# Two quantised feed-forward weights prepared in quarters instead of whole, in a four-stage transformer kernel

## The chip, the cores and the metric

The kernel runs on one core of a Trainium2 chip. A core has a matrix engine (TensorE, PE in the profile; its weight loads are PEld), a vector engine (VectorE, DVE), an activation engine (ScalarE, ACT), a general engine (GpSimd, POOL) and a queue that issues DMAs (SyncE, SP). Each engine works through its own queue in order and waits on semaphores for the others. The metric is the device time of one execution in microseconds (us); lower is better. Before the change the median of three runs is 962.21 us (961.23 to 963.15).

## What is computed

Four stages run over x of shape (8, 512, 256), each with a residual and a layer norm:

```python
x = layernorm(x + retention(x, past_kv, W_qkv, ...))         # 16 heads, group norm
x = layernorm(x + ffn(x, W_fc, ln_w, ln_b, W_proj))          # the change is here
x = layernorm(x + linear_attention(x, Wq, Wk, Wv, ...))
x = layernorm(x + mixture_of_experts(x, w_router, wi, wo))

def absmean(W):                          # W_fc is (1024, 256), W_proj is (256, 1024)
    gamma = mean(abs(W)) + 1e-6
    return sign(W / gamma) * minimum(round(abs(W / gamma)), 1)      # -1, 0 or 1

def ffn(x, W_fc, ln_w, ln_b, W_proj):
    h = gelu(x @ absmean(W_fc).T)
    h = layernorm(h, ln_w, ln_b)
    return h @ absmean(W_proj).T
```

Before feed-forward can run, each of its weights is summed in absolute value over all its elements (for gamma), turned into -1, 0 and 1 by two thresholds at half of gamma, and transposed. W_proj is also scaled by ln_w, has its column means taken away, and gives a bias from ln_b: the layer norm is folded into the weight.

## The kernel before, in words

One batch has 512 tokens in four blocks (chunks) of 128. Its retention stage is `stage_a1`, group norm and residual `stage_a2`, feed-forward `stage_b` and `stage_bn`, linear attention `stage_c1` and `stage_c2`; experts follow for two groups of four batches. The stages of different batches are interleaved.

The order is not written by hand. Every stage is a generator, and `interleave` advances the one whose next step may begin first by a planned clock. `op(engine, cost, t, ...)` enters an instruction with a cost and the time at which its inputs are expected; it is placed in the first free stretch of that engine's planned time. Two engine names matter here: `DVS` is VectorE working from SBUF only, for which the planner also books a "port" that `POOL` books too; `DVE` books VectorE alone. `pe(cost)` advances the planned time of TensorE, `need(t)` waits in the plan until `t`, and `later(t)` hands on a time. The planned times set the order of the instructions in each engine's queue, and nothing else: on the chip the semaphores decide. Where the plan leaves TensorE idle for over 1.4 us, `interleave` enters spare matmuls on the identity and a table (line 294), whose output nobody reads.

The preparation of feed-forward is the generator `prepare_ffn`, which runs beside `stage_a1` of batch 0. It issues one DMA of 1 MB for W_fc into one half of the tile `prepare`, one for W_proj into `pr_w`, and two for ln_w and ln_b (`lnwb`, line 678). `threshold` plans the arrival by its last argument (24.0 and 27.0 us), sums the whole weight by one VectorE reduction into a column `fc_t` or `pr_t`, adds over the partitions by a matmul with ones (line 647) and makes the two thresholds by three small instructions (lines 651 to 655). `ternary` makes the quantised weight by two VectorE instructions over 128x2048 elements: a compare (`is_lt`) and a compare with a subtraction (`is_gt`, `subtract`). Then come 16 transposes of each weight on TensorE (line 692 `fc_tp`, line 705 `pr_tp`) with copies by ScalarE, the product with ln_w on VectorE (`prT`), the bias (`pr_bias`, line 721), the means (`pr_mean`, line 729) and the subtraction of the means from `prT` on VectorE.

In `stage_a1` of a batch, TensorE makes q and k (`qk_ps`, line 880) and v (`v_ps`, line 904), and then for each of the four chunks: scores (`sc`, line 928), a transpose of k (`kd_tp`, line 935), the chunk's output (`r_ps`, lines 948 to 961) and the state's update (`st_ps`, line 970). Between the scores and the output stands the decay mask: three of four score banks are multiplied on VectorE and one is copied by ScalarE and multiplied on POOL (`masked`, tiles `scm`). `past_bd`, the state carried in, is made by four VectorE instructions (lines 612 and 617) and `gnp`, the spread group-norm weights, by four more (lines 623 and 624). The last chunk's statistics (`gn_st`) begin `stage_a2`. `stage_a1` of batch 1, whose first instructions on TensorE are the transposes of x at line 348, comes after that of batch 0 and after `prepare_ffn`. `prepare_l1`, the generator behind it, transposes the weights of the third stage (line 801, `l_tp`), clears two padding tiles on POOL (`pad`) and issues small DMAs.

DMAs are all on SP's queue, in the order of the plan. At the start they are: identity, x of batch 0, wqkv, the tables `cst`, `past`, two for `gn`, W_fc, W_proj, two for `lnwb`, x of batch 1, four small vectors of the third stage and the first of its weights.

Of the kernel before, what the change touches and what calls it, by code (L numbers as in the profile page):

```python
# [11 lines left out]
F32 = mybir.dt.float32  # L12
# [3 lines left out]
ALU = mybir.AluOpType  # L16
AX = mybir.AxisListType
# [3 lines left out]
P = 128  # L21
B, S, D = 8, 512, 256
NC = S // P
NK = D // P
# [57 lines left out]
def tile_layers(ctx: ExitStack, tc: tile.TileContext, ins, out, at):  # L82
# [6 lines left out]
    def bc(ap, axis, n):  # L89

        shape = list(ap.shape)
        return ap.unsqueeze(axis).to_broadcast(shape[:axis] + [n] + shape[axis:])
# [83 lines left out]
    def op(engine, cost, t, fn, *args, use=None, drop=None, bank=None, **kw):  # L176


        if engine in (GELU, EXP):
            cost += 0.0 if engine == Plan.loaded else TABLE  # L180
            engine, Plan.loaded = ACT, engine
        users = [engine]
        if engine in (DVS, POOL):
            users.append("port")
        engine = users[0] = {DVS: DVE, POOLD: POOL}.get(engine, engine)
        t = t + HOP
        if use is not None:
            t = max(t, take(use) + HOP)
        if engine != SP:
            length = max(cost - OVERLAP[engine], 0.05)  # L190
            found = False
            while not found:
                found = True
                for user in users:
                    for a, b in Plan.busy[user]:
                        if t + length <= a:
                            break
                        if b > t:
                            t, found = b, False
            for user in users:  # L200
                bisect.insort(Plan.busy[user], (t, t + length))
                while Plan.busy[user][0][1] < Plan.t - 30.0:
                    Plan.busy[user].pop(0)
        Plan.count += 1
        heapq.heappush(Plan.events, (t, Plan.count, lambda: fn(*args, **kw)))  # L205
        t += cost
        if drop is not None:
            give(drop, t)
        if bank is not None:
            release(bank, t)  # L210
        return t
# [5 lines left out]
    def pe(cost):  # L217


        start = max(Plan.now, Plan.t)  # L220
        if start - Plan.now > 1.5:
            Plan.slow = start + (1.5 if start - Plan.now < 3.0 else 8.0)
        cost += min(max(Plan.slow - start, 0.0) / 2, cost)
        Plan.now = Plan.t = start + cost
        return Plan.now + PE_OUT
# [12 lines left out]
    def need(t, n=1):  # L238

        while True:  # L240
            r = max(t + HOP_PE, sorted(Plan.banks)[n - 1] + HOP if n else 0.0)
            yield "pe", r if r < HELD else Plan.t + 0.5
            if not n or sorted(Plan.banks)[n - 1] <= Plan.t + 1e-6:
                return
# [324 lines left out]
    with ExitStack() as stages:  # L569
# [15 lines left out]
        def dma(t, out, in_):  # L585
            op(SP, 0.0, t, nc.sync.dma_start, out=out, in_=in_)
# [49 lines left out]
        prbias = fb.tile([P, D], F32, name="prbias")  # L636
        lnwb = fb.tile([P, 2, NF], F32, name="lnwb")

        def threshold(name, w, t):

            tot = fb.tile([P, 1], F32, name=f"{name}_t")
            t = op(
                DVE, 2.3, t, V.tensor_reduce, tot, w, AX.X, ALU.add, apply_absolute_value=True
            )
            yield from need(t)
            ps = bank(f"{name}_ps")
            T.matmul(ps[:, 0:1], ones, tot, start=True, stop=True)
            half = fb.tile([P, 2], F32, name=f"{name}_h")

            def halves():  # L650
                nc.vector.tensor_scalar(
                    half[:, 1:2], ps[:, 0:1], 1.0 / (FF * D), 1e-6, ALU.mult, ALU.add
                )
                nc.vector.tensor_scalar(half[:, 0:1], half[:, 1:2], 0.5, None, ALU.mult)
                nc.vector.tensor_scalar(half[:, 1:2], half[:, 1:2], -0.5, None, ALU.mult)

            return half, op(DVE, 0.5, pe(0.2), halves, bank=ps)

        def ternary(q, w, half, t):
            t = op(DVS, 1.3, t, V.tensor_scalar, q, w, half[:, 1:2], None, ALU.is_lt)  # L660
            return op(
                DVS, 2.35, t, V.scalar_tensor_tensor, q, w, half[:, 0:1], q, ALU.is_gt, ALU.subtract
            )

        def prepare_ffn():

            big = fb.tile([P, 2, FF * D // P], F32, tag="big", bufs=1, name="prepare")
            w_fc, q_fc = (big[:, i].rearrange("p (n c) -> p n c", n=NF) for i in range(2))
            dma(0.0, w_fc, ins["L0_ffn_W_fc"].rearrange("(n p) c -> p n c", p=P))
            w_pr, q_pr = (  # L670
                wk.tile([P, NK, FF], F32, tag="b8", bufs=B8, name=f"pr_{i}") for i in "wq"
            )
            dma(0.0, w_pr, ins["L0_ffn_W_proj"].rearrange("(m p) c -> p m c", p=P))

            def vectors():
                for j, k in enumerate(("L0_ffn_ln_w", "L0_ffn_ln_b")):
                    with nc.allow_non_contiguous_dma(reason="a vector of 1024, once"):
                        nc.sync.dma_start(
                            out=lnwb[:, j, :], in_=ins[k].rearrange("(n p) -> p n", p=P)
                        )  # L680

            op(SP, 0.0, 0.0, vectors)
            half, t = yield from threshold("fc", big[:, 0], 24.0)
            ready = ternary(big[:, 1], big[:, 0], half, t)
            half, t = yield from threshold("pr", w_pr.rearrange("p m c -> p (m c)"), 27.0)
            ready_pr = ternary(*(x.rearrange("p m c -> p (m c)") for x in (q_pr, w_pr)), half, t)
            for k in range(NK):
                for n4 in range(NF // 4):
                    yield from need(ready)
                    ps = bank("fc_tp")  # L690
                    for n in range(4):
                        T.transpose(
                            ps[:, n * P : (n + 1) * P],
                            q_fc[:, n4 * 4 + n, k * P : (k + 1) * P], ident,
                        )
                    fc_done = op(
                        ACT, 0.6, pe(0.46), A.copy, fcT[:, k, n4 * 512 : (n4 + 1) * 512], ps, bank=ps
                    )
            raw = big[:, 0].rearrange("p (f d) -> p f d", f=NF)
            for n2 in range(NF // 2):  # L700
                yield from need(ready_pr)
                ps = bank("pr_tp")
                for n in range(2):
                    for m in range(NK):
                        T.transpose(
                            ps[:, (n * 2 + m) * P : (n * 2 + m + 1) * P],
                            q_pr[:, m, (n2 * 2 + n) * P : (n2 * 2 + n + 1) * P], ident,
                        )
                t = op(
                    ACT, 0.6, pe(0.46), A.copy,  # L710
                    raw[:, n2 * 2 : n2 * 2 + 2, :].rearrange("p n d -> p (n d)"), ps, bank=ps,
                )
            give("b8", Plan.now, 2)
            w = op(
                DVS, 2.3, t, V.tensor_tensor, prT[:, :, :D], raw, bc(lnwb[:, 0, :], 2, D), ALU.mult
            )
            op(DVE, 0.1, w, V.memset, prT[:, :, D : D + 1], 1.0 / FF)
            yield from need(t)
            acc = bank("pr_bias")
            for f in range(NF):  # L720
                T.matmul(
                    acc[:, :D], lnwb[:, 1, f : f + 1].to_broadcast([P, P]), raw[:, f, :],
                    start=(f == 0), stop=(f == NF - 1),
                )
            op(ACT, 0.4, pe(3.5), A.copy, prbias, acc[:, :D], bank=acc)
            yield from need(w)
            acc = bank("pr_mean")
            for f in range(NF):
                T.matmul(acc[:, :D], ones, prT[:, f, :D], start=(f == 0), stop=(f == NF - 1))
            mean = wk.tile([P, D], F32, tag="ex", bufs=EX, name="pr_mean_s")  # L730
            t = op(
                ACT, 0.4, pe(3.5), A.activation, mean, acc[:, :D], AF.Copy, scale=1.0 / FF,
                use="ex", bank=acc,
            )
            t = op(
                DVS, 2.3, t, V.tensor_tensor, prT[:, :, :D], prT[:, :, :D], bc(mean, 1, NF),
                ALU.subtract, drop="ex",
            )
            yield later(t)
            return t  # L740

# [1078 lines left out]
```

## Time and profile before

| what | value |
|---|---|
| median of three runs | 962.21 us |
| profiled execution, time | 959.53 us |
| profiled execution, span in the trace | 957.8 us |
| mean granted clock of TensorE | 0.977 |
| busy in 0 to 24 us: PE, DVE, ACT, POOL | 18.38, 6.49, 5.97, 8.21 us |
| busy in 24 to 48 us: PE, DVE, ACT, POOL | 22.68, 20.65, 7.32, 5.78 us |
| busy in 60 to 100 us (40 us): PE, DVE | 38.85, 21.14 us |
| spare matmuls in the whole span | 164 passes, 43.3 us |

The span is what the trace covers; the time of the same execution is 1.7 us longer. A matmul of 32-bit floats appears as two passes in the rows, so "x12" spare rows are six instructions. In a timeline a row gives the start in us from the span's start, how long the group lasted, the engine, the line, the operation, the tiles written and read, the shape, the number of instructions and, in brackets, how long the engine stood idle before it and what released it. L205 is the line of the helper that enters a planned instruction, so the tile names say which it is. A row of the DMA issues ends in the size and the time from issue to landing.

### The profile page before, as it was taken

The numbers are of one execution on the slowest core, as the hardware profiler recorded it, in microseconds if no ns is written. First come the engines' busy times: TensorE is split into PE (matmuls) and PEld (weight loads), VectorE is DVE, ScalarE is ACT, GpSimd is POOL, SyncE is SP. The second block draws the span as 40 slices with busy tenths as digits, with TensorE's granted clock in tenths as the row PEclk, the third lists the DMA queues.
The fourth block names the chain that finished last, engine by engine and source line by source line (L and its number), as shares of the span: only waits on it lengthen the run. The fifth ranks groups of instructions, "written<-read, shape, count | busy, mean of one in ns | idle before, by whom it ended". The sixth has DMA issues, their size and how long they took to land. (4 is left out here: it accounts for less than half of the span.)

```text
span 957.8 us, 18818 instructions
## 1 busy us (share of the span) xinstructions
PE 902.4 (94%) x7704; PEld 706.9 (74%) x7704; DVE 614.9 (64%) x1506; ACT 445.2 (46%) x862; POOL 397.2 (41%) x404
## 2 busy tenths in 40 slices
PE   7999999999999998999998999979999999999892
PEld 4777777777777786777676766658686898999891
DVE  2855446788668678767889788857765953513224
ACT  2337266356834943671755155632655534122213
POOL 3246446432554543362436134362365223253333
PEclk9999999999999999999999899989999999999895
DMA  6030000002000100200020010001503356339742
GB/s 209 8 111 2 2 1 2 2 1 67 1 2 23 46 1 1 67 2 1 1 68 1 1 43 4 2 1 45 190 15 108 122 172 207 80 92 369 244 123 101
DMA packets 49542, 60.68 MB, mean 63 GB/s; under 512 B 5585, under 2 KB 44689, under 8 KB 49457
## 3 DMA queue, kind: packets, MB, share of 16 engines
q1 hardware_dynamic: 45600, 53.92, 16.9%
q0 software_dynamic: 3856, 5.57, 3.0%
q8 instruction: 60, 0.98, 0.4%
q14 instruction: 26, 0.20, 0.1%
HBM read 43.76 MB, written 15.73 MB: 62 GB/s over the span
## 5 line engine op out<-in xcount | busy, mean ns | idle before, releaser
L1125 PE MATMUL pr_ps<-prT,fT 128*128 128x257 f32 x512 | 117.1, 382 | 0.3 <-ACT scm L205 0.3
L1125 PEld LDWEIGHTS pr_ps<-prT,fT 128*128 128x128 f32 x512 | 95.5, 189 | 16.6 <-issue 1.9
L205 POOL TENSOR_TENSOR fsq<-fsq,fsf 128x512 f32<-128x512 f32 x56 | 72.6, 1296 | 30.6 <-ACT fsf L205 28.1
L1517 PE MATMUL wo_ps<-e_hT,wo 128*128 128x160 f32 x512 | 75.2, 305 | 0.0
L1488 PE MATMUL wi_ps<-xsT,wi 128*128 128x160 f32 x512 | 74.8, 300 | 0.0
L205 ACT ACTIVATE e_hT<-wi_ps 128x480 f32<-128x480 f32 (+1 forms) x48 | 25.3, 527 | 105.4 <-PE wi_ps L1488 105.4
L1517 PEld LDWEIGHTS wo_ps<-e_hT,wo 128*128 128x128 f32 x512 | 71.9, 193 | 1.1 <-issue 0.6
L1488 PEld LDWEIGHTS wi_ps<-xsT,wi 128*128 128x128 f32 x512 | 70.7, 190 | 0.5 <-issue 0.2
L205 DVE TENSOR_TENSOR hm<-hs,cst 128x512 f32<-128x512 f32 x96 | 60.0, 676 | 15.6 <-PE hs L1264 15.6
L205 POOL TENSOR_TENSOR ln_rs<-ln_rs,mhalf 128x4 f32<-128x4 f32 x32 | 33.4, 1045 | 84.2 <-DVE ln_rs L205 84.2
L205 POOL TENSOR_TENSOR scm<-scm,cst 128x512 f32<-128x512 f32 x32 | 43.7, 1367 | 54.2 <-ACT scm L205 54.1
L205 DVE TENSOR_TENSOR scm<-sc,cst 128x512 f32<-128x512 f32 x96 | 60.1, 676 | 8.6 <-PE sc L928 8.6
L1205 PE MATMUL qk_ps<-l1T,x2T 128*128 128x512 f32 x128 | 61.7, 603 | 0.0
L205 POOL TENSOR_TENSOR hm<-hm,cst 128x512 f32<-128x512 f32 x32 | 40.9, 1279 | 48.2 <-ACT hm L205 48.2
L205 DVE STREAM_TRANSPOSE hT<-pad 128x512 f32<-128x512 f32 x64 | 59.3, 958 | 2.1 <-ACT pad L205 1.4
L205 POOL DMA_INDIRECT y_d<-eo,srci x21 | 32.5, 1549 | 66.2 <-ACT eo L205 33.5
L880 PE MATMUL qk_ps<-xT,wqkv 128*128 128x512 f32 x128 | 59.4, 606 | 0.0
L1096 PE MATMUL fc_ps<-x1T_l,fcT 128*128 128x512 f32 x128 | 53.2, 415 | 2.8 <-DVE x1T_l L205 1.5
L1096 PE MATMUL fc_ps<-x1T_h,fcT 128*128 128x512 f32 x128 | 50.2, 392 | 0.0
L205 ACT ACTIVATE x<-x,ln_nb,ln_rs 128x256 f32<-128x256 f32 x64 | 33.2, 589 | 31.5 <-DVE ln_nb L205 31.4
L294 PE MATMUL spare<-cst,cst_ident 128*128 128x256 f32 x164 | 43.3, 415 | 0.0
L205 ACT ACT_TABLE_LOAD x33 | 42.3, 1283 | 1.3 <-PEq L1806 0.7
(257 smaller groups left out, 1990.2 us busy)
## 6 DMA issues: line engine op xcount, KB each, us to landing
wi<-in_L_ffn_wi SPq DMA_DIRECT2D x13, 1024.0 KB, 6.7
wo<-in_L_ffn_wo SPq DMA_DIRECT2D x13, 1024.0 KB, 7.6
x<-in_L_attn_x SPq DMA_DIRECT2D x8, 512.0 KB, 3.9
x_d<-a SPq DMA_DIRECT2D x8, 512.0 KB, 3.0
y_d<-a SPq DMA_DIRECT2D x8, 512.0 KB, 4.1
z<-y_d SPq DMA_DIRECT2D x8, 512.0 KB, 6.2
out<-z SPq DMA_DIRECT2D x8, 512.0 KB, 3.1
prepare<-in_L_ffn_W_fc SPq DMA_DIRECT2D x1, 1024.0 KB, 11.3
```

The source lines that it names most:

```text
L205: heapq.heappush(Plan.events, (t, Plan.count, lambda: fn(*args, **kw)))
L294: T.matmul(ps[:, :256], ident, cst[:, :256], start=True, stop=True)
L880: T.matmul(ps, wqkv[:, k, which * D + m * P : which * D + (m + 1) * P], xT[:, k, :], start=(k == 0), stop=(k == NK - 1),)
L1096: T.matmul(ps, fcT[:, k, f * P : (f + 1) * P], x[:, k, :], start=(k == 0 and x is low), stop=(k == NK - 1 and x is high),)
L1125: T.matmul(acc[:, : D + 1], hT[:, f, c * P : (c + 1) * P], prT[:, f, :], start=(f == 0), stop=(f == NF - 1),)
L1205: T.matmul(qk, x2T[:, k, cs], l1T[:, k, 0:2, :].rearrange("p a d -> p (a d)"), start=(k == 0), stop=(k == NK - 1),)
L1488: T.matmul(ps[:, f * CAP : (f + 1) * CAP], wi[:, k, (f3 + f) * P : (f3 + f + 1) * P], x[:, k, es], start=(k == 0), stop=(k == NK - 1),)
L1517: T.matmul(ps[:, m * CAP : (m + 1) * CAP], wo[:, f, m * P : (m + 1) * P], hT[:, f, :], start=(f == 0), stop=(f == NF - 1),)
```

## The change

W_fc is loaded by four DMAs of 256 KB (two blocks of 128 rows each) and W_proj by four (half a row block each). Each quarter is summed by a reduction of its own into one of four columns, and the sum over partitions accumulates four matmuls with ones instead of one. The quantising runs as four pairs of 128x512 instructions, the product with ln_w and the subtraction of the means as four instructions each. The planned arrivals are 12.0, 13.5, 14.7 and 16.0 us for the quarters of W_fc (24.0 for the whole before) and 17.0 to 20.0 for W_proj (27.0 before); costs in the plan are cut accordingly. The transposes of W_fc run block of four first, and each waits in the plan for the quarter that it reads.

Because the plan decides the order, the built queues differ as follows, all in the first two batches. TensorE: the sums of W_fc stand before `v_ps` instead of behind the first chunk's spare matmuls; the sums of W_proj and the transposes of W_fc stand behind the first chunk's scores, the transposes of W_proj behind the second's; bias and means stand before the third chunk's scores instead of the fourth's; one block of third-stage transposes stands before batch 1's x transposes. Spare instructions by chunk are 2, 0, 6 and 5 instead of 6, 5, 5 and 7, and 2 are added in batch 1. VectorE: three sums of W_fc stand before `past_bd`, the fourth before `kT`, all of W_fc's quantising and the sums of W_proj before the first masks. SP: the eight quarter DMAs stand in place of the two.

```diff
--- before.py
+++ after.py
@@ -636,15 +636,20 @@
         prbias = fb.tile([P, D], F32, name="prbias")
         lnwb = fb.tile([P, 2, NF], F32, name="lnwb")
 
-        def threshold(name, w, t):
-
-            tot = fb.tile([P, 1], F32, name=f"{name}_t")
-            t = op(
-                DVE, 2.3, t, V.tensor_reduce, tot, w, AX.X, ALU.add, apply_absolute_value=True
-            )
+        def threshold(name, parts, ts):
+
+            tot = fb.tile([P, len(parts)], F32, name=f"{name}_t")
+            for i, (part, t) in enumerate(zip(parts, ts)):
+                t = op(
+                    DVE, 0.61, t, V.tensor_reduce, tot[:, i : i + 1], part, AX.X, ALU.add,
+                    apply_absolute_value=True,
+                )
             yield from need(t)
             ps = bank(f"{name}_ps")
-            T.matmul(ps[:, 0:1], ones, tot, start=True, stop=True)
+            for i in range(len(parts)):
+                T.matmul(
+                    ps[:, 0:1], ones, tot[:, i : i + 1], start=(i == 0), stop=(i == len(parts) - 1)
+                )
             half = fb.tile([P, 2], F32, name=f"{name}_h")
 
             def halves():
@@ -654,23 +659,37 @@
                 nc.vector.tensor_scalar(half[:, 0:1], half[:, 1:2], 0.5, None, ALU.mult)
                 nc.vector.tensor_scalar(half[:, 1:2], half[:, 1:2], -0.5, None, ALU.mult)
 
-            return half, op(DVE, 0.5, pe(0.2), halves, bank=ps)
-
-        def ternary(q, w, half, t):
-            t = op(DVS, 1.3, t, V.tensor_scalar, q, w, half[:, 1:2], None, ALU.is_lt)
-            return op(
-                DVS, 2.35, t, V.scalar_tensor_tensor, q, w, half[:, 0:1], q, ALU.is_gt, ALU.subtract
-            )
+            return half, op(DVE, 0.5, pe(0.5), halves, bank=ps)
+
+        def ternary(qs, ws, half, t):
+
+            ends = []
+            for q, w in zip(qs, ws):
+                e = op(DVS, 0.36, t, V.tensor_scalar, q, w, half[:, 1:2], None, ALU.is_lt)
+                ends.append(op(
+                    DVS, 0.64, e, V.scalar_tensor_tensor, q, w, half[:, 0:1], q, ALU.is_gt,
+                    ALU.subtract,
+                ))
+            return ends
 
         def prepare_ffn():
 
             big = fb.tile([P, 2, FF * D // P], F32, tag="big", bufs=1, name="prepare")
             w_fc, q_fc = (big[:, i].rearrange("p (n c) -> p n c", n=NF) for i in range(2))
-            dma(0.0, w_fc, ins["L0_ffn_W_fc"].rearrange("(n p) c -> p n c", p=P))
             w_pr, q_pr = (
                 wk.tile([P, NK, FF], F32, tag="b8", bufs=B8, name=f"pr_{i}") for i in "wq"
             )
-            dma(0.0, w_pr, ins["L0_ffn_W_proj"].rearrange("(m p) c -> p m c", p=P))
+            fc_rows = ins["L0_ffn_W_fc"].rearrange("(n p) c -> p n c", p=P)
+            pr_rows = ins["L0_ffn_W_proj"].rearrange("(m p) c -> p m c", p=P)
+            fours = range(4)
+            for i in fours:
+                dma(0.0, w_fc[:, 2 * i : 2 * i + 2], fc_rows[:, 2 * i : 2 * i + 2])
+
+            def half_row(x, i):
+                return x[:, i // 2, i % 2 * 512 : (i % 2 + 1) * 512]
+
+            for i in fours:
+                dma(0.0, half_row(w_pr, i), half_row(pr_rows, i))
 
             def vectors():
                 for j, k in enumerate(("L0_ffn_ln_w", "L0_ffn_ln_b")):
@@ -680,13 +699,15 @@
                         )
 
             op(SP, 0.0, 0.0, vectors)
-            half, t = yield from threshold("fc", big[:, 0], 24.0)
-            ready = ternary(big[:, 1], big[:, 0], half, t)
-            half, t = yield from threshold("pr", w_pr.rearrange("p m c -> p (m c)"), 27.0)
-            ready_pr = ternary(*(x.rearrange("p m c -> p (m c)") for x in (q_pr, w_pr)), half, t)
-            for k in range(NK):
-                for n4 in range(NF // 4):
-                    yield from need(ready)
+            parts = [[big[:, k, i * 512 : (i + 1) * 512] for i in fours] for k in range(2)]
+            half, t = yield from threshold("fc", parts[0], [12.0, 13.5, 14.7, 16.0])
+            ready = ternary(parts[1], parts[0], half, t)
+            parts = [[half_row(w, i) for i in fours] for w in (w_pr, q_pr)]
+            half, t = yield from threshold("pr", parts[0], [17.0, 18.0, 19.0, 20.0])
+            ready_pr = max(ternary(parts[1], parts[0], half, t))
+            for n4 in range(NF // 4):
+                for k in range(NK):
+                    yield from need(ready[2 * n4 + 1])
                     ps = bank("fc_tp")
                     for n in range(4):
                         T.transpose(
@@ -711,9 +732,11 @@
                     raw[:, n2 * 2 : n2 * 2 + 2, :].rearrange("p n d -> p (n d)"), ps, bank=ps,
                 )
             give("b8", Plan.now, 2)
-            w = op(
-                DVS, 2.3, t, V.tensor_tensor, prT[:, :, :D], raw, bc(lnwb[:, 0, :], 2, D), ALU.mult
-            )
+            for f in range(0, NF, 2):
+                w = op(
+                    DVS, 0.62, t, V.tensor_tensor, prT[:, f : f + 2, :D], raw[:, f : f + 2],
+                    bc(lnwb[:, 0, f : f + 2], 2, D), ALU.mult,
+                )
             op(DVE, 0.1, w, V.memset, prT[:, :, D : D + 1], 1.0 / FF)
             yield from need(t)
             acc = bank("pr_bias")
@@ -732,10 +755,12 @@
                 ACT, 0.4, pe(3.5), A.activation, mean, acc[:, :D], AF.Copy, scale=1.0 / FF,
                 use="ex", bank=acc,
             )
-            t = op(
-                DVS, 2.3, t, V.tensor_tensor, prT[:, :, :D], prT[:, :, :D], bc(mean, 1, NF),
-                ALU.subtract, drop="ex",
-            )
+            for f in range(0, NF, 2):
+                e = op(
+                    DVS, 0.62, t, V.tensor_tensor, prT[:, f : f + 2, :D], prT[:, f : f + 2, :D],
+                    bc(mean, 1, 2), ALU.subtract, drop="ex" if f == NF - 2 else None,
+                )
+            t = e
             yield later(t)
             return t
 
```

## Prediction

> **What bounds the kernel now.** I read the page's busy shares first, then the timeline of all engines over the first 60 us (the change touches nothing later), then the DMA issues with their time to landing, and last the places where TensorE waited. The first line says which engine to follow:
>
> ```profile
> PE 902.4 (94%) x7704; PEld 706.9 (74%) x7704; DVE 614.9 (64%) x1506; ACT 445.2 (46%) x862; POOL 397.2 (41%) x404
> ```
>
> TensorE is the bound, so the change is worth what it moves TensorE's queue by the time the second batch begins (the x transposes at 56.81), since from there on the queues of both programs are almost the same. But "busy" includes spare matmuls, which only pass time. Timeline:
>
> ```profile
> 18.69 1.15 PE L928 MATMUL sc<-qz,kT 32*128 32x256 f32 x16
> 20.05 2.76 PE L294 MATMUL spare<-cst,cst_ident 128*128 128x256 f32 x12
> 20.51 2.27 DVE L205 TENSOR_REDUCE fc_t<-prepare 128x1 f32<-128x2048 f32 x1
> 24.45 1.29 DVE L205 TENSOR_SCALAR prepare<-prepare,fc_h 128x2048 f32<-128x2048 f32 x1
> 25.77 2.35 DVE L205 SCALAR_TENSOR_TENSOR prepare<-prepare,fc_h 128x2048 f32<-128x2048 f32 x1
> 27.01 2.32 PE L294 MATMUL spare<-cst,cst_ident 128*128 128x256 f32 x10
> 30.47 0.35 PE L647 MATMUL pr_ps<-pr_t,cst 128*128 128x1 f32 x2 [1.13 <-DVE pr_t L205]
> 36.45 2.32 PE L294 MATMUL spare<-cst,cst_ident 128*128 128x256 f32 x10
> 51.13 2.29 DVE L205 TENSOR_TENSOR prT<-prT,pr_mean_s 128x2048 f32<-128x2048 f32 x1 [5.60 <-ACT pr_mean_s L205]
> 51.69 2.89 PEld L294 LDWEIGHTS spare<-cst,cst_ident 128*128 128x128 f32 x14 [0.33 <-issue]
> 52.50 2.06 POOL L205 TENSOR_TENSOR scm<-scm,cst 128x512 f32<-128x512 f32 x1 [11.94 <-ACT scm L205]
> 56.81 1.09 PE L348 MATMUL tp<-cst_ident,x 128*128 128x128 f32 x8
> ```
>
> The reader should see four gaps, one behind each of the four score blocks, filled by 46 spare passes of 0.23 us (10.7 us) plus 1.13 us of plain waiting: that is the reserve a better order could use. The DMA issues say when the weights are there:
>
> ```profile
> prepare<-in_L_ffn_W_fc SPq DMA_DIRECT2D x1, 1024.0 KB, 11.3
> pr_w<-in_L_ffn_W_proj SPq DMA_DIRECT2D x1, 1024.0 KB, 13.3
> gn<-in_L_attn_gn_weight SPq DMA_DIRECT2D x1, 8.0 KB, 8.6
> gn<-in_L_attn_gn_bias SPq DMA_DIRECT2D x1, 8.0 KB, 8.8
> ```
>
> Issued at 4.29 and 4.77, they land at 15.6 and 18.1, and VectorE takes them at 20.51 and 28.04. The slack is 5 to 10 us; the change spends it.
>
> **The loads.** Two DMAs become eight. In the compiled order each hardware DMA waits for the landing of the one eight issues earlier. So the four fc quarters leave at 4.3, 4.8, 5.4 (x landed) and 7.3 (wqkv landed, 1.64+5.6), the pr quarters at 9.1, 9.6, 11.8 and 12.5 (cst, past and the two gn). None is late: the engines are on gn's small packets until about 12. A 1 KB packet takes 46 ns in the trace and each of 16 engines has 16 per quarter, 0.74 us, so going back from 15.6 the fc quarters land at about 13.4, 14.1, 14.9, 15.6. The pr quarters follow by 18.3 and are first wanted near 23. Behind them on SP, the lnwb vectors (4.98 and 4.14 us of issue) move from 5.4 to 13.4, landing by about 25, wanted at 35; x of batch 1 goes from 14.7 to 22.5, wanted at 56; l1w to about 28, wanted at 56. All free. The Trainium skill (DMA: Bandwidth & Descriptors, Measured) says to batch DMAs to at least 1 MiB, and its anatomy section puts about 2 us fixed on each. Were that serial, three more would put the last fc quarter at 21.6, the estimate for the kernel about 967. The trace says otherwise: x, wqkv and cst, issued 0.5 us apart, kept the DMA engines 0.92 to 1.15 busy from 3.5 to 8 us without a hole, so I take nothing. The bounds are 14.6 and 18.1; it costs nothing below 16.5, and 1:1 above.
>
> **VectorE, costed in quarters.** From the 128x128 and 128x2048 rows, a 512-wide compare is about 0.44 (0.23 and 1.29), a select 0.70 (0.29 and 2.35), a reduction 0.6 a step. With 0.03 between dependents and 0.09 overlap otherwise, a pair steps 1.08, a weight 4.3 us against 3.67 now; four reductions 2.42 against 2.28, four folds 2.45 against 2.28. VectorE pays 0.65+0.65+0.3+0.35 = 1.9 us more, most of it now on the path.
>
> **TensorE's new order, walked through.** After the q and k projections (15.3, unchanged) stand the four fc sums, which were behind the first spares. Everything behind them, v_ps and the first scores included, waits. VectorE reduces quarters 1 to 3 by 15.6, then past_bd (1.02, moved behind them) by 16.6, then quarter 4 by 17.2; kT, once free at 13.6 and 15.4, follows. The last fc sum ends at 17.7, v_ps 21.3, and the first scores start at 21.2 instead of 18.69: **2.5 late**.
> VectorE: kT to 18.5, halves 19.0, ternary 23.35, pr sums 25.75, masks of block 0 27.6. TensorE has 4 spare passes, then the pr sums to 26.25, fc transposes (1.94) 28.1, r of block 0 29.8, state 30.5, scores of block 1 at 30.4 (now 25.66): **4.7 late**.
> VectorE: pr halves 28.1, ternary 32.4, statistics and state 33.15, masks 35.0, folds 37.4. TensorE: pr transposes in the gap behind scores 1, to 33.7 (they wait for pr_q); r and state of block 1 to 36.8 (now 35.17): **1.6 late, with pr_tp already done**.
> pr_bias and pr_mean (3.6 each) to 43.8, scores of block 2, 12 spare passes to 47.9. VectorE subtracts the mean 44.3 to 46.75, masks to 48.6; r 2 ends at 50.1. Scores 3 to 51.9, 10 spare passes to 54.1, r 3 ends at 56.25 (now 56.88): **0.6 early**.
> The same in one ledger: 20 spare passes fewer, -4.65; the 1.13 wait and 0.2 of mask waits, -1.3; against that waits of about 2.05 before the fc sums, 2.3 around the pr sums, 0.8 at pr_tp and r 1: -0.8, the same within my rounding.
>
> **Behind 56 us.** One l1 transpose block (0.5) moves ahead of batch 1 and a later one goes: nil by 90 us. A spare pair (0.92) is put before the x1 transposes, where TensorE now waits in pieces of 0.16 for ACT's x; it fits there. Elsewhere the queues agree, and SP, POOL and ACT swap neighbours that have microseconds of slack (pad's two memsets pass ahead of mask 3 on POOL, done at 51.6; the mask is wanted at 52.6).
>
> **Two costs the trace does not show outright.** First the port of VectorE and POOL. In the row at 52.50 POOL's mask product took 2.06 instead of 1.27, ending 1.1 us after VectorE's single 2.29 us subtraction let go. Now the subtraction is four pieces and POOL's mask of block 2 asks at 45.6, in the third. If POOL gets in at the seam, VectorE's last piece waits 1.2 us, block 2's masks end at 49.8, and r 2 slips by 0.85. Zero is the other end. No row shows who wins at such a seam; at 38.82 a VectorE piece did stand until POOL was through, so I take 0.85 as a little likelier.
> Second the clock. These rows are from batch 2's transposes:
>
> ```profile
> 203.09 0.67 PE L1082 MATMUL tp<-cst_ident,x 128*128 128x128 f32 x4 [1.89 <-DVE scm L205]
> 203.80 6.58 PE L294 MATMUL spare<-cst,cst_ident 128*128 128x256 f32 x22
> ```
>
> After a wait of only 1.89 us the spare passes took 0.37 on average for 0.23; the granted clock was half for 3.4 us. The Trainium skill (TensorE: Matmul & The Clock Gate, HAM oscillation) allows idle gaps up to about 3.4 us; by it my gaps (0.85 before the last fc sum, four pieces of 0.2 to 0.5 around the pr sums, with 0.35 us one-column matmuls between) are harmless. By the row the second group, 2.3 us with little in it, may trip it. Half clock for 3.4 us from 26 would stretch the fc transposes, but VectorE's ternary hides part: 1.2 at r 1. Half for 6.8 us, which the granted clock shows at four other waits, costs about 2.7. I take none, as the one-column matmuls cut the gap, at 0.3 for either.
>
> **Sum.** -0.6 + 0.85 = +0.25 us. The profiled execution has a span of 957.8 and a time of 959.53, 2.7 below the median of the runs; I add the difference to the median 962.21: **962.5 us**.
>
> **Rivals.**
> 1. *The port is no matter* (0.3): -0.6, or down to -1.5 if the last quarter lands early and the overlaps are as good as in the masks: 961.2. For it: POOL may lose the race. Against: the lock seen twice.
> 2. *The clock falls* (0.28): at the pr sums TensorE has about 2.3 us with almost no work, the window trips, and transposes and scores run at half rate for 3.4 to 6.8 us. With the port that is -0.6+0.85+1.2 = +1.5 to -0.6+0.85+2.7 = +3.0: 963.7 to 965.2, slower. It decides once a window is as empty as that at 203.
> 3. *The last fc quarter is late* (0.07): at 18.1, where both weights land now, +1.5, 964.0 with the port.
> 4. *The plan's own gain comes through* (0.05): if the ternaries step at the plan's 1.0 us and all waits at the sums are filled, about -2.5, 959.7.
> The forecast itself has 0.3.
>
> A measurement of this kernel tells about 0.2% from no change, 1.9 us: faster means below 960.3, slower above 964.1. Faster gets rival 4 and a tail of 1, 0.12; slower most of 2, half of 3 and what I overlooked on a path that is now serial through VectorE, 0.30; same 0.58. The range 960.2 to 965.6 takes in all but the far ends of 2 and 4.
>
> **What would show it.** Right: the last fc reduction at 16.5 to 17.5, first scores at 21 to 21.5, r 3 done near 56 to 57, half the spare passes gone, first 60 us of PE busy lower with the same end. Wrong: a fc reduction starting after 18 (the loads), a granted clock under 1.00 in the stretch 20 to 40 (rival 2), VectorE's four subtractions without a hole and POOL's mask ending after them (rival 1), or batch 1's transposes starting before 54.5 (rival 4).

## The result, and the profile after

The kernel after takes 963.73 us in the median (961.27 to 964.96, 20 executions); the kernel before, beside it, 961.00 (959.36 to 963.64, 20 executions). The ratio, which is that of the mean times, is 1.0021, 95% interval 1.0012 to 1.0030: about 2.0 us slower (the medians lie 2.7 apart). The forecast was 962.5 us, +0.25 against the kernel before. The time lies in the range, at its slow side, because the range was wide: the likeliest case was too kind by 1.8 us.

Executions of one kernel spread over 4 to 5 us, about half of it with their mean granted clock (over 75 executions of the kernel before, 0.57 us for each 0.001), so I read the place of a loss in the traces and its size in the ratios. The profiled execution after is 964.39 us (span 962.6, clock 0.972), 1.15 above the mean of its runs; that of before, at 959.53, was 1.7 below. The 4.8 us between the spans overstate the change.

First the page's busy shares of the kernel after: nearly the same work, 3.8 us more of it on VectorE. Below, fc and proj stand for W_fc and W_proj, and the *ternary* of a weight is its quantising, a compare and a select.

```profile
PE 903.2 (94%) x7700; PEld 708.5 (74%) x7700; DVE 618.7 (64%) x1530; ACT 445.3 (46%) x862; POOL 396.9 (41%) x404
```

Then I set each TensorE instruction that both programs have beside its twin. The shift is -0.3 us when q and k are done, +1.8 at the first scores (20.46 against 18.69), +2.8 at batch 1's x transposes (59.58 against 56.81), and after up to 3.3 in batch 1 it is back at +2.80 from 93 us on and between +2.8 and +2.9 until 890 us. So it is made in the first 60 us. The timeline there, TensorE first:

```profile
16.59 0.38 PE L650 MATMUL fc_ps<-fc_t,cst 128*128 128x1 f32 x2 [1.00 <-DVE fc_t L205]
...
20.46 1.15 PE L953 MATMUL sc<-qz,kT 32*128 32x256 f32 x16
...
24.85 0.92 PE L650 MATMUL pr_ps<-pr_t,cst 128*128 128x1 f32 x4 [2.00 <-DVE pr_t L205]
25.95 1.18 PE L650 MATMUL pr_ps<-pr_t,cst 128*128 128x1 f32 x4 [0.17 <-DVE pr_t L205]
26.99 3.65 PE L713 MATMUL fc_tp<-cst_ident,prepare 128*128 128x128 f32 x16
...
34.87 1.91 PE L726 MATMUL pr_tp<-cst_ident,pr_q 128*128 128x128 f32 x16
...
59.58 1.04 PE L348 MATMUL tp<-cst_ident,x 128*128 128x128 f32 x8
```

Up to the first scores all goes as forecast, 0.7 us earlier than forecast even. Then TensorE stands 2.00 us for VectorE's sums, and the fc transposes take 3.65 us instead of 1.94: half speed. The stretch 20 to 40 us of the windows (busy us of PE, PEld, DVE, ACT, POOL with their counts, then the granted clock, DMA share, GB/s) says it in its clock of 0.83; in the trace the half clock lasts from 25.6 to 32.4 us.

```profile
20.00:40.00 20.00, 17.68 (x171) 14.95 (x170) 19.16 (x36) 7.34 (x16) 5.33 (x5) 0.83 0.09 25
```

VectorE and POOL in the same trace, at the fc ternary's last two pairs, at the product with ln_w and at the mean subtraction:

```profile
17.65 0.15 DVE L656 TENSOR_SCALAR fc_h<-fc_ps 128x1 f32<-128x1 f32 x1
...
21.10 0.75 DVE L205 SCALAR_TENSOR_TENSOR prepare<-prepare,fc_h 128x512 f32<-128x512 f32 x1
...
21.77 0.48 DVE L205 TENSOR_SCALAR prepare<-prepare,fc_h 128x512 f32<-128x512 f32 x1
...
22.28 1.83 DVE L205 SCALAR_TENSOR_TENSOR prepare<-prepare,fc_h 128x512 f32<-128x512 f32 x1
...
22.30 1.27 POOL L205 TENSOR_TENSOR scm<-scm,cst 128x512 f32<-128x512 f32 x1 [7.23 <-ACT scm L205]
...
24.03 2.45 DVE L205 TENSOR_REDUCE pr_t<-pr_w 128x1 f32<-128x512 f32 x4
...
36.53 2.68 DVE L205 TENSOR_TENSOR prT<-prepare,lnwb 128x512 f32<-128x512 f32 x4
...
36.62 1.45 POOL L205 TENSOR_SCALAR qz<-qd,cst 128x256 f32<-128x256 f32 x1
...
46.69 3.57 DVE L205 TENSOR_TENSOR prT<-prT,pr_mean_s 128x512 f32<-128x512 f32 x4 [5.37 <-ACT pr_mean_s L205]
...
48.06 1.66 POOL L205 TENSOR_TENSOR scm<-scm,cst 128x512 f32<-128x512 f32 x1 [9.99 <-ACT scm L205]
```

A select takes 0.75 us, the last of the four 1.83: POOL's mask product started beside it and was through first. The same happens in the subtraction, 3.57 us in four pieces where one instruction took 2.29. The whole fc ternary takes 5.86 us (18.17 to 24.03, where the next reduction begins; before 3.62), that of proj 4.82 (28.75 to 33.57).

### The profile page after: what moved, and what is told of

Its sections match the earlier page's. It is cut to its first block, busy times and chain, and to the rows that moved or that the text cites. A ratio compares the mean times of both kernels' runs of the same rounds, so it can differ in the third digit from the quotient of the medians.

```text
span 962.6 us, 18843 instructions
## 1 busy us (share of the span) xinstructions
PE 903.2 (94%) x7700; PEld 708.5 (74%) x7700; DVE 618.7 (64%) x1530; ACT 445.3 (46%) x862; POOL 396.9 (41%) x404
## 5 line engine op out<-in xcount | busy, mean ns | idle before, releaser
L1150 PEld LDWEIGHTS pr_ps<-prT,fT 128*128 128x128 f32 x512 | 95.5, 189 | 16.6 <-issue 1.9
L205 POOL TENSOR_TENSOR scm<-scm,cst 128x512 f32<-128x512 f32 x32 | 41.6, 1299 | 54.4 <-ACT scm L205 54.3
L205 POOL TENSOR_SCALAR pad<-pad,lamv 128x128 f32<-128x128 f32 x32 | 12.0, 374 | 74.3 <-DVE pad L205 74.2
```

The source lines that it names most:

```text
L1150: T.matmul(acc[:, : D + 1], hT[:, f, c * P : (c + 1) * P], prT[:, f, :], start=(f == 0), stop=(f == NF - 1),)
```

## The experiments

So there are three suspects: the half clock, the pairs of the ternaries on VectorE's chain, and POOL's entry between pieces. My theory was that the half clock made most of the loss (1 to 2 us), the rival that VectorE's chain did. All kernels of the table but the last have the order of the kernel after on every engine, the added spares apart. The last fc sum ends up to 1.6 us apart in their profiled executions (16.54 to 18.16), so I compare the *path*: from the first threshold instruction (`fc_h`), which follows the last fc sum, to batch 1's x transposes. After: 59.58 - 17.65 = 41.93 us. Each path is one execution; the ratio is that of all.

| kernel | half clock in 17 to 40 us | proj ternary ends, from `fc_h` | path | against after | ratio to before |
|---|---|---|---|---|---|
| after | 25.6 to 32.4 | 15.92 | 41.93 | | 1.0021 [1.0012, 1.0030] |
| + spares before the proj sums | none | 16.82 | 41.55 | -0.4 | 1.0027 [1.0016, 1.0038] |
| subtraction whole | 26.3 to 33.1 | 15.94 | 40.99 | -0.9 | 1.0017 [1.0006, 1.0028] |
| proj ternary whole | 27.8 to 34.6 | 14.78 | 42.22 | +0.3 | 1.0020 [1.0010, 1.0030] |
| proj ternary whole + spares | none | 14.77 | 39.66 | -2.3 | 1.0010 [1.0000, 1.0020] |
| fc ternary whole | none | 14.58 | 39.31 | -2.6 | 1.0014 [1.0002, 1.0026] |
| fc ternary whole + spares | none | 13.70 | 38.42 | -3.5 | 1.0004 [0.9993, 1.0016] |
| both ternaries whole | 19.1 to 22.5 | 12.55 | 37.56 | -4.4 | 0.9986 [0.9977, 0.9996] |
| everything whole but loads and sums | none | 12.56 | 36.44 | -5.5 | 0.9963 [0.9952, 0.9973] |
| before, with the new estimates only | 21.0 to 24.4 | 12.37 | 36.68 | | 0.9985 [0.9977, 0.9993] |

**The clock held.** Five spare instructions ahead of the sums of W_proj:

```diff
             ps = bank(f"{name}_ps")
+            if name == "pr":
+                for _ in range(5):
+                    T.matmul(ps[:, :256], ident, cst[:, :256], start=True, stop=True)
```

> The kernel after with five more spare instructions on TensorE (ten passes, 10 x 0.23 = about 2.3 us) queued in front of the four one-column sums of the projection; nothing else moves. Clock theory: TensorE is then busy in the 2.0 us in which it waits for VectorE at 22.9 to 24.9 us, the half clock at 25.6 to 32.4 us is not there (granted clock 1.00 from 20 to 40 us), the fold of the feed-forward weights takes 1.9 us instead of 3.65, and all of the later work, which stands 2.8 us behind the kernel before from 97 us on, stands 1.0 to 2.0 us behind: time 1 to 2 us below the kernel after, ratio to the kernel before 1.000 to 1.001. Rival (VectorE's order and its port alone make the loss, and the slow fold is hidden beside the projection's ternary): the clock comes back or not, the later work moves by less than 0.4 us, ratio 1.002.

The clock is 1.00 and the fc transposes (the fold, in the expectations) take 1.95 us, and the time does not move: ratio 1.0027, path -0.4. My theory fell here. The timeline of this kernel says why:

```profile
23.64 2.32 PE L651 MATMUL pr_ps<-cst,cst_ident 128*128 128x256 f32 x10
...
27.74 1.95 PE L716 MATMUL fc_tp<-cst_ident,prepare 128*128 128x128 f32 x16
...
33.07 0.89 PE L729 MATMUL pr_tp<-cst_ident,pr_q 128*128 128x128 f32 x4
...
33.54 1.33 POOL L205 TENSOR_TENSOR scm<-scm,cst 128x512 f32<-128x512 f32 x1 [7.68 <-ACT scm L205]
...
33.79 1.63 DVE L205 SCALAR_TENSOR_TENSOR pr_q<-pr_w,pr_h,pr_q 128x512 f32<-128x512 f32 x1
...
35.82 1.53 PE L729 MATMUL pr_tp<-cst_ident,pr_q 128*128 128x128 f32 x12 [1.86 <-DVE gn_st L205]
```

TensorE comes to the proj transposes early and then stands 1.86 us, until the last piece of `pr_q` is there at 35.42. (The row names `gn_st`, which follows that piece on VectorE.) And because scores 1 now come earlier, POOL's mask of block 1 meets that last select, 1.63 us instead of 0.75. The gain on TensorE was waited away. (An estimate from these rows: without that meeting TensorE could have begun at 15.9 us after `fc_h` and not at 17.2, so the half clock alone was worth at most 1.3 us. No run has the spares without the meeting and with both ternaries in pairs.)

**The subtraction whole.**

```diff
-            for f in range(0, NF, 2):
-                e = op(
-                    DVS, 0.62, t, V.tensor_tensor, prT[:, f : f + 2, :D], prT[:, f : f + 2, :D],
-                    bc(mean, 1, 2), ALU.subtract, drop="ex" if f == NF - 2 else None,
-                )
-            t = e
+            t = op(
+                DVS, 2.24, t, V.tensor_tensor, prT[:, :, :D], prT[:, :, :D], bc(mean, 1, NF),
+                ALU.subtract, drop="ex",
+            )
```

> The kernel after with the mean subtracted by one instruction, as in the kernel before, instead of four; all other instructions keep their order. Port theory: GpSimd's causal selection cannot come in between pieces, the subtraction ends after 2.3 us instead of 3.6, and block 3's r and everything after it comes 0.9 to 1.3 us earlier, ratio to before about 1.001. Rival (the four-piece subtraction costs nothing, since the selection that came in early is one that would be waited for later anyway): less than 0.3 us, ratio 1.002. The half clock at 25.6 to 32.4 us stays under either.

VectorE's subtraction and POOL's mask product of block 2 in its timeline:

```profile
47.41 2.29 DVE L205 TENSOR_TENSOR prT<-prT,pr_mean_s 128x2048 f32<-128x2048 f32 x1 [5.37 <-ACT pr_mean_s L205]
...
48.77 2.06 POOL L205 TENSOR_TENSOR scm<-scm,cst 128x512 f32<-128x512 f32 x1 [9.98 <-ACT scm L205]
```

Now it is POOL that is held (2.06 us) and not VectorE. The path is 0.94 us shorter, as expected; the ratios, 1.0017 against 1.0021, cannot tell that from nothing by themselves.

**Both ternaries whole**, as one compare and one select over 2048 columns each; sums, product and subtraction stay in quarters. (The cut below leaves out the calls that pass the whole weights.)

```diff
-            for q, w in zip(qs, ws):
-                e = op(DVS, 0.36, t, V.tensor_scalar, q, w, half[:, 1:2], None, ALU.is_lt)
-                ends.append(op(
-                    DVS, 0.64, e, V.scalar_tensor_tensor, q, w, half[:, 0:1], q, ALU.is_gt,
-                    ALU.subtract,
-                ))
+            t = op(DVS, 1.45, t, V.tensor_scalar, q, w, half[:, 1:2], None, ALU.is_lt)
+            e = op(
+                DVS, 2.55, t, V.scalar_tensor_tensor, q, w, half[:, 0:1], q, ALU.is_gt, ALU.subtract
+            )
```

> The kernel after with each ternary as one comparison and one selection over all 2,048 columns, as in the kernel before, instead of four pairs; sums, folds and order of all else stay. If the pairs cost what their rows say (4.8 us against 3.7 us for the whole, and 1.1 us more where GpSimd came in at the last selection of the feed-forward one), both ternaries end some 1.1 us sooner each, the projection's ternary ends near 31 us instead of 33.6, TensorE's wait for the projection's sums is 2 us shorter and the clock may not fall at all: the later work comes 1.5 to 2.8 us earlier, ratio 0.9995 to 1.0005. Rival (the first fold of the feed-forward weights, which now waits for the whole ternary, or scores 1 sets the time): less than 0.5 us, ratio 1.002.

Ratio 0.9986: 3.4 us (0.0035 x 961) below the kernel after, and below the kernel before: more than the 1.5 to 2.8 us expected. The rows: the two fc instructions and the two of proj in 3.64 us each, and TensorE at the proj sums and at the proj transposes without a wait.

```profile
19.23 1.29 DVE L205 TENSOR_SCALAR prepare<-prepare,fc_h 128x2048 f32<-128x2048 f32 x1
...
20.55 2.35 DVE L205 SCALAR_TENSOR_TENSOR prepare<-prepare,fc_h 128x2048 f32<-128x2048 f32 x1
...
25.39 0.95 PE L650 MATMUL pr_ps<-pr_t,cst 128*128 128x1 f32 x8
...
31.52 1.91 PE L725 MATMUL pr_tp<-cst_ident,pr_q 128*128 128x128 f32 x16
```

The clock fell even here, elsewhere: at 19.1 us for 3.4 us, after TensorE had waited 0.32 and 1.13 us for the fc sums. This execution (961.01 us) is among the slower of its kernel, whose median is 959.26; whether the clock fell in the others is not known.

**One ternary at a time, with and without the spares**, to see how chain and clock act together. The edit is the one above for one weight, and the five spares of the first experiment.

> The kernel after with the projection's ternary alone as one comparison and one selection; the feed-forward one stays in four pairs, all orders stay. Two-stage theory: the half clock at 25.6 to 32.4 us stays, and with it TensorE reaches the projection's transposes at 34.9 us whatever VectorE does; the ternary ends at 32.4 instead of 33.6 us and nothing comes of it: less than 0.4 us, ratio 1.0017 to 1.0022. Rival (VectorE alone sets the time): 1.0 to 1.3 us earlier, ratio about 1.001.

> The one before (projection's ternary whole) with the five spare instructions on TensorE in front of the projection's sums, so that the clock is held as well. Two-stage theory: clock and projection's pairs lie side by side at about 34 us, each covers the other's removal, and both removed together give what neither gives alone: transposes at 32.5 us instead of 34.9, everything after it 1.9 to 2.5 us earlier than in the kernel after, ratio 0.9995 to 1.0003. Rival (the clock costs nothing in any setting): the same as the run without the fill, within 0.3 us.

In the traces both came as the two-stage theory said. The proj ternary whole alone: ended 1.1 us sooner, nothing gained, because TensorE at half clock reaches the transposes at 36.78 in any case (`fc_h` at 19.27 in that execution). With the clock held as well, TensorE waits 0.30 us at 32.66 and the path is 2.3 us shorter. In the ratios the pair is 1.0020 and 1.0010, with intervals that overlap: 1.0 us of the trace's 2.6, not clear of noise, and less than the 0.9995 to 1.0003 expected of the second. So the two-stage account rests on the traces.

The timeline of the kernel without the spares:

```profile
28.60 3.65 PE L715 MATMUL fc_tp<-cst_ident,prepare 128*128 128x128 f32 x16
...
36.78 1.91 PE L728 MATMUL pr_tp<-cst_ident,pr_q 128*128 128x128 f32 x16
```

And of the one with them:

```profile
26.87 1.94 PE L718 MATMUL fc_tp<-cst_ident,prepare 128*128 128x128 f32 x16
...
32.66 1.94 PE L731 MATMUL pr_tp<-cst_ident,pr_q 128*128 128x128 f32 x16 [0.30 <-ACT scm L205]
```

The fc transposes at half speed (3.65) and at full (1.94) stand ahead of the proj transposes in both.

> The kernel after with the feed-forward ternary alone as one comparison and one selection over 2,048 columns; the projection's stays in four pairs, all orders stay. Two-stage theory (the four pairs and GpSimd's cut-in at the last of them lengthen VectorE's chain by 2.2 us ahead of the projection's sums, and that same lateness leaves TensorE idle at 22.9 us and brings the half clock): from the threshold to the end of the ternary 3.6 us instead of 5.8; TensorE's wait for the sums gone, clock 1.00 from 20 to 35 us; the transposition of block 0 of the next stage 2.0 to 2.7 us earlier than in the kernel after, ratio to before 0.9990 to 1.0000. Rival (the projection's pairs are the larger part of the 3.4 us that whole ternaries gave): 0.5 to 1.2 us, ratio 1.001 to 1.0016.

In the trace it did what was expected: the fc ternary 3.63 us, the wait of 2.00 us gone, no half clock before 100 us, path -2.6. It did not reach 4.4, because POOL's mask of block 1 came upon the last select of the proj ternary (1.63 us), as in the first experiment. In the ratios it gained 0.7 us only, and the expected ratio was missed. I supposed that the half clock came back in its other executions:

> The version with the feed-forward ternary alone whole, and the five spare instructions in front of the projection's sums added. That version stood 2.6 us ahead of the kernel after in its trace, but only 0.7 us in the medians. If the half clock comes back in its other executions (its profiled one had none before 100 us and was among its five fastest of 14), the spares hold it off in all: median 960.3 to 961.0, ratio 1.0000 to 1.0006, and no cluster near 963.5. Rival (the spread is made elsewhere in the run, and the spares only end after the last sum is ready): ratio 1.0012 to 1.0020, the spread as before.

The ratio fell from 1.0014 to 1.0004, as expected for a returning half clock, but the interval (0.9993 to 1.0016) holds the rival too, and the executions still spread from 960.8 to 965.9, five of 14 between 963.1 and 964.4, as the rival said. In its trace POOL's mask missed the proj ternary, and the path is 0.9 us shorter than without the spares. Whether the unprofiled executions of the fc-only kernel lose their clock stays open.

**The new estimates without the quarters.** The kernel before with two numbers changed:

```diff
-            half, t = yield from threshold("fc", big[:, 0], 24.0)
+            half, t = yield from threshold("fc", big[:, 0], 16.0)
 ...
-            half, t = yield from threshold("pr", w_pr.rearrange("p m c -> p (m c)"), 27.0)
+            half, t = yield from threshold("pr", w_pr.rearrange("p m c -> p (m c)"), 19.0)
```

> The kernel before, whole loads and whole instructions, with the plan told that the weights arrive at 16 and 19 us instead of 24 and 27; the order of the work on every engine then is about that of the kernel after. It shows what the new estimate is worth without the quarters. If the estimate is what makes room (the quarters and their seams are what costs): 0.3 to 1 us faster than before, ratio 0.999 to 1.000, clock at full speed from 20 to 40 us. Rival (the order that follows from the early estimate is itself what leaves TensorE without work near 23 us, so that the clock falls): half clock near 25 us and 1 to 2 us slower, ratio 1.001 to 1.002.

Ratio 0.9985, 1.4 us faster than before, a little more than the theory asked. The clock fell for 3.4 us in its profiled execution, as the rival said; that execution is the slowest of its 23 (963.91 us, median 959.25), so what the others did is not known. The order that comes of the early estimate pays by itself.

**The loads alone.** The kernel before with eight quarter DMAs in place of two (the cut shows those of W_fc; those of W_proj are made likewise).

```diff
-            dma(0.0, w_fc, ins["L0_ffn_W_fc"].rearrange("(n p) c -> p n c", p=P))
+            fc_rows = ins["L0_ffn_W_fc"].rearrange("(n p) c -> p n c", p=P)
+            for i in range(4):
+                dma(0.0, w_fc[:, 2 * i : 2 * i + 2], fc_rows[:, 2 * i : 2 * i + 2])
```

> The kernel before with the two weights loaded in quarters and nothing else changed: sums, quantising, folding and the plan's estimates stay. Theory: SyncE's queue takes six more issues that delay nothing, and no one waits for the weights in the old order, so the time is that of the kernel before: ratio 0.9993 to 1.0007. Rival (the shorter transfers or the later issues of the loads queued behind them push the arrival of past and position data and with them the first scores): 0.5 to 1.5 us slower, ratio 1.0005 to 1.0015.

0.9991 [0.9981, 1.0000], just faster than the expected band: no loss. The DMA issues of the kernel after show the quarters behind one another (8.6 and 6.5 us from issue to landing, where the whole took 11.3 and 13.3):

```profile
prepare<-in_L_ffn_W_fc SPq DMA_DIRECT2D x4, 256.0 KB, 8.6
pr_w<-in_L_ffn_W_proj SPq DMA_DIRECT2D x4, 256.0 KB, 6.5
```

**Quarters for loads and sums, everything else whole**: the edits of the subtraction and both ternaries, and the product with ln_w as one instruction again.

> The kernel after with quarters kept for the loads and the sums alone: both ternaries, the scaling by the norm's weights and the mean subtraction are one instruction each over all columns, as before; all orders stay. If the gains of whole ternaries (3.4 us) and of the whole subtraction (0.9 us in the trace) add, it stands 4.0 to 4.6 us ahead of the kernel after: ratio 0.997 to 0.998, faster than both kernels. Rival (the subtraction's gain is taken up by another wait once the ternaries are whole, as the timed runs of the subtraction alone, 0.4 us, may say): ratio 0.9983 to 0.9988, as with whole ternaries alone.

Median 957.52 us, ratio 0.9963: 3.5 us faster than the kernel before and 5.6 than the kernel after, where the path says 5.5. The gains add, to more than the 4.0 to 4.6 us expected; the product in one piece is new here and was not tried alone. What the quarters are worth where they belong is the step from "new estimates only" to here: 0.9963 against 0.9985, 2.1 us, and the traces agree: the thresholds begin at 19.02 us instead of 21.00, because the sum starts at 14.34 on the first quarter and not at 17.60 on the whole. (In these two executions the last of W_fc landed at 16.4 and 17.6 us, so part of the 2.0 us in the traces is the landing itself.) First the kernel with the estimates only, then this one:

```profile
17.60 2.29 DVE L205 TENSOR_REDUCE fc_t<-prepare 128x1 f32<-128x2048 f32 x1 [3.82 <-DMA prepare<-in_L_ffn_W_fc]
```

```profile
14.34 2.05 DVE L205 TENSOR_REDUCE fc_t<-prepare 128x1 f32<-128x512 f32 x3 [13.48 <-DMA prepare<-in_L_ffn_W_fc]
...
44.40 2.76 PE L294 MATMUL spare<-cst,cst_ident 128*128 128x256 f32 x12
...
55.46 1.04 PE L348 MATMUL tp<-cst_ident,x 128*128 128x128 f32 x8
```

**Bias and means later.** The 12 spare passes at 44.40 asked to be used:

```diff
-            yield from need(t)
+            yield from need(t + 4.0)
             acc = bank("pr_bias")
```

> The version with quarters for loads and sums alone and everything else whole, and one thing more: the plan is told that the norm's bias and mean sums (two times 3.6 us on TensorE) are wanted 4 us later, which puts them behind scores 2, where twelve spare passes (2.8 us) stood, and puts the causal factors of block 2 ahead of the mean subtraction on VectorE; some small steps of the first layer's start move too. Theory (from 43 to 56 us TensorE waits for the causal factors and not for the sums; work in place of the spares is free): block 0 of the next stage 2.0 to 3.0 us earlier than in the version without it, ratio to before 0.9935 to 0.9950. Rival (the subtraction then holds up the group norm and state of block 2, or the moved small steps of the next layer cost as much later): 0 to 1 us, ratio 0.9955 to 0.9970.

Near the edit the theory held: batch 1's transposes start at 52.37 instead of 55.46, 3.1 us earlier. The time is 976.87 us, ratio 1.0152 [1.0129, 1.0175]. The plan orders everything that follows from the times it has by then, and from batch 1 on TensorE's queue has another order: 182 spare passes in the span instead of 148, and at the transposes of line 348 19.8 us of waits for VectorE's `a` instead of 9.8. So the local gain is shown in one trace, the expected ratio was missed by theory and rival alike, and what the gain is worth at the end is not testable by this edit.

## Why the prediction was right or wrong

**The loads: right.** The first fc sum starts at 12.84, the last ends at 16.54 (forecast 17.2, "16.5 to 17.5"). Quarters cost nothing. The trace shown is the earliest of ten that have these loads and sums: in the others the last sum ends at 16.6 to 18.2 us. The 2 us fixed cost that I took from the Trainium skill (DMA: Bandwidth & Descriptors, Anatomy of one DMA) is given there for DMAs issued by GpSimd; these are issued by SyncE, and their fc quarters landed at 12.82, 13.57, 14.31 and 15.00 us, 0.7 apart, so it was not paid once for each in turn. Behind them on the queue my walk was too slow: the two `lnwb` issues took 0.38 us each and not 4.98 and 4.14, and x of batch 1 left at 14.33 and not at 22.5. Nothing waited for these.

**TensorE's walk to the first scores: right**, 20.46 against 21.2 forecast.

**"VectorE pays 0.65+0.65+0.3+0.35 = 1.9 us more": the step that failed.** Measured, 5.86 - 3.62 = 2.2 for the fc ternary, 4.82 - 3.67 = 1.2 for proj, 0.2 for the proj sums and 0.4 for the product (2.68 against 2.28): 4.0 us, the subtraction not counted. Two terms of it were off. "A pair steps 1.08" should be 1.19 (0.49 for the compare and 0.75 for the select, where I had put 0.44 and 0.70 between a 128-wide and a 2048-wide row): 0.9 us over both ternaries. And I priced POOL's entry at a seam in one place, the subtraction, though the fc ternary has seven seams and its last pair was to stand at 22.3 to 23.35: block 0's mask on POOL, which begins 1.84 us after the scores, was due at 23.0 by my own walk, some 0.3 us behind that pair's seam and within the walk's error. In the trace it was there at 22.30, at the seam. That is 1.1 us that the walk has nowhere.

**"If POOL gets in at the seam, VectorE's last piece waits 1.2 us": right.** 3.57 us, 1.28 over the whole instruction; taking it away gave 0.9 on the path, where I had put 0.85. Rival 1 is out.

**"I take none" for the clock: wrong in the event, and less wrong in the price.** The window at the proj sums did trip the clock, at its place and for 6.8 us. Between the row at 203 us (half clock after 1.89 us) and the rule of the Trainium skill (TensorE: Matmul & The Clock Gate, HAM oscillation: gaps up to about 3.4 us are harmless) the row was right: 2.00 us, with one-column matmuls behind them, were enough. (Over the 22 passes of that row a spare pass took 0.30 us; my 0.37 is that of its first twelve.) Rival 2 named the event, and its 963.7 to 965.2 holds the median, but by a sum that the runs do not bear out: with the clock held alone, 0.4 us came back in the trace and nothing in the ratio. I had the ternary hide "part" of the half rate; in truth the proj ternary and TensorE's slow stretch end within 1.3 us of one another (33.57 and 34.87), and each covers the other. The fall at the proj sums is a price of the longer chain: when the fc ternary ended in time, it was not there.

**Rival 3** (a late last quarter) did not happen in this execution. **Rival 4** was given 0.05 and -2.5 us; the gain is there, -1.4 by the estimates and -3.5 with the sums in quarters, but only where the ternaries are not cut.

**"Behind 56 us: nil by 90 us": off by 0.5.** The block of third-stage transposes (l1) that moves ahead adds 0.5 us, and where it is missing later the shift does fall, from 3.24 to 2.80 at 93 us. But in between q and k of batch 1 wait 0.60 us for `xT`, and the first chunk's output waits 0.97 us for POOL's mask where it waited 0.61.

**The sum.** Forecast -0.6 + 0.85 = +0.25 at the end of the last chunk's output (r 3); the trace shows it at 59.15 against 56.88, +2.27. The 2.0 us between are in place when the mean sums end: 46.2 us against 43.8 forecast. They are as much as VectorE's 4.0 us exceed the 1.9.

## What to carry to other kernels

Cut into pieces what lets a consumer start before its input is whole, here loads and sums; leave whole what feeds a step that needs all of it, since every piece pays its start again on the serial chain and gives another engine a place to step in. When the path passes to another engine, cost that engine's chain instruction by instruction, and look at each seam for who is due then. Where two late things end side by side, take both away in one experiment before calling either harmless.

## What the runs showed of the hardware

- Against one 2048-wide instruction POOL was held (2.06 us for a mask product of 1.27); against pieces POOL got in at a seam and VectorE was held (1.83, 1.63 and 3.57 us for 0.75, 0.75 and 2.29). It need not be the first seam: at 36.62 us POOL's `qz` (1.45 us for 0.48) passed one seam of the product's pieces and got in at the second, where it held the third piece to 0.88 us for 0.68.
- The granted clock fell to half after waits of 2.00 us (after) and 1.85 us (new estimates only) and, with one-column matmuls between, of 0.32 and 1.13 us (both ternaries whole); after 0.18 and 1.13 us at the same place (proj ternary whole) it did not. With spares in the gap at the proj sums it did not fall in three of three traces, one of which has no such gap without them. Holding off a half clock of 6.8 us gained nothing in the ratio where another chain ended nearly as late.
- Six more DMA issues at the head of one queue cost nothing: the loads alone in quarters gave 0.9991 [0.9981, 1.0000].
